# Layer 0's attention half a unit behind its maxima, in program order, with loads by need

## The chip, the cores and the metric

The kernel runs on one core of one Trainium2 chip. Times are device microseconds of one execution. A core has five engines with a queue each: TensorE (PE: matrix products, with its weight loads shown as PEld), VectorE (DVE), ScalarE (ACT), GpSimd (POOL) and SyncE (SP, which issues transfers). Products land in PSUM, a small memory of eight banks for each of 128 partitions; all other tiles lie in SBUF. An engine executes its own queue in order and waits for the others by semaphores.

## The reference

The program is a sequence of two transformer layers over x of 2 batches, 1024 tokens and 128 channels. Each part is added to x after a layernorm of x:

```
x = x + L0_attn(layernorm(x))   # 8 heads of 128, queries and keys through a latent of 32, rotary part of 32
x = x + L0_ffn(layernorm(x))    # a shared expert and the best 2 of 8 experts for each token
x = x + L1_attn(layernorm(x))   # 16 heads of 8, rotated, causal
x = x + L1_ffn(layernorm(x))    # 2 of 8 experts for each batch
```

The change lies in L0_attn. It is, with c_q and c_kv of 32 channels:

```
c_q, c_kv = h @ W_DQ + b_DQ, h @ W_DKV + b_DKV
q = [c_q @ W_UQ + b_UQ, c_q @ W_QR + b_QR];  k = [c_kv @ W_UK + b_UK, h @ W_KR + b_KR]
attn = softmax(q @ k.T / sqrt(160));  out = (attn @ v) @ W_O + b_O,  v = c_kv @ W_UV + b_UV
```

The kernel never builds the heads of 128 channels. It multiplies the weights with each other first: W_UQ with W_UK into `g`, a map from c_q to 64 channels per head, and W_UV with W_O into `w_vo`. Scores are then products over 64 channels, and values have 32.

## The kernel before

**Layer 0's attention** is cut into four units: 2 batches by 2 groups of 4 heads, `i = 0..3`. A unit has two passes over its 1024 by 1024 scores.

- `maxima0(i)` (L612) computes scores with queries on the partitions. A tile `sc` (L621) covers 128 queries, 512 keys and 2 heads: two matrix products on two halves of the rows of PE, then one `tensor_reduce` on DVE (L628). There are 32 tiles and 32 yields in a unit. After every 16 tiles the maxima are split into three bf16 parts on DVE (L640 to L653), and `rows` (L655) turns them into rows: 16 small products, and a copy to `mr` on ACT.
- `attend0(i)` (L670) computes the scores again, with keys on the partitions (L692), adds the negated maxima by a product with ones (L698), takes the exponential on ACT (L703), adds up the exponentials for the denominator (`sum`, L708 and L711: on POOL, for the last unit on DVE) and multiplies them with the values (`values`, L721) into `ud`. It also has 32 tiles and 32 yields, in two halves `c`. At the end of a half, `end` (L733) multiplies the sums with ones (`den`), copies `ud` and `den` on ACT, and puts six items into the list `late`: four divisions, a blank and `add`, the product with `w_vo` that goes into x. `run` (L677) takes one item before each yield.

In what follows a step is one yield of these generators.

Tiles `sc`, and all small products of this stage, share a PSUM pool `ps` of three buffers of two banks each (L466).

**Ahead of the units** stand `prepare(0)` (L545: layernorm, transposes, `cq`, `key2`, `val`, `cc`) and `queries(0)` (L594: two products of 33 rows, copied on ACT to `q2`). Before them in the program come the loads, the constants (masks, `tri`, `thr`, `ids` and others), and the products of weights: `gp` (L507), `vo` (L517) and `bo` (L527, with `bv` and `b_o` giving the output's bias `b_all`). x is loaded in four pieces by SP (L65), then the expert weights `wall` (L491 to L495); the other weights go through ACT's queue, the first five ahead of `w_up`, `w_o` and `g`.

**The order.** Five stages run (L779). Stage i takes a step of `maxima0(i)`, a step of `attend0(i - 1)` and a step of `more()` in turn, until all have ended; so stage 0 has maxima alone and stage 4 attention alone. `more()` prepares the second batch in stage 1, and makes the next queries, a piece every four steps. In stages 0 to 3 the order is fixed on PE alone; the order of the other engines, and everything ahead of stage 0, is up to a scheduler that plans with estimated times. In stage 4 PE, DVE, POOL and SP follow the program (`IN_ORDER`, L42), and `ahead` goes on by one step beside each: `route(0)` (L287), the choice of experts for the first batch, two of its yields at a time, then the gathers `get(0)` (L449) of the first rows for the experts. After that come the experts, layer 1's attention and its experts, which the change does not touch.

Of the kernel before, what the change touches and what calls it, by code (L numbers as in the profile page):

```python
# [13 lines left out]
F32 = mybir.dt.float32  # L14
# [7 lines left out]
P = 128  # L22
# [3 lines left out]
NE = 8  # L26
# [23 lines left out]
def two_layers(ctx: ExitStack, tc: tile.TileContext, a: dict, out: bass.AP):  # L50
# [13 lines left out]
    for i in range(4):  # L64
        nc.sync.dma_start(  # L65
            x[:, 4 * i : 4 * i + 4, :],
            a["h"][4 * i * P : 4 * (i + 1) * P, :].rearrange("(n p) d -> p n d", p=P),
        )

    ident = const.tile([P, P], F32, name="ident")  # L70
# [3 lines left out]

    mask_st = const.tile([P, P], BF16, name="mask_st")
    nc.gpsimd.memset(mask_st, 0.0)
    nc.gpsimd.affine_select(
        out=mask_st, in_=mask_st, compare_op=ALU.is_ge, fill=MASKED,
        base=0, pattern=[[-1, P]], channel_multiplier=1,
    )  # L80
    mask_ts = const.tile([P, P], BF16, name="mask_ts")
    nc.gpsimd.memset(mask_ts, 0.0)
    nc.gpsimd.affine_select(
        out=mask_ts, in_=mask_ts, compare_op=ALU.is_ge, fill=MASKED,
        base=0, pattern=[[1, P]], channel_multiplier=-1,
    )
    mhalf = const.tile([P, NT], F32, name="mhalf")
    nc.gpsimd.memset(mhalf, -0.5)

    rev_i = const.tile([P, NE], I32, name="rev_i")  # L90
    nc.gpsimd.iota(rev_i, pattern=[[-1, NE]], base=NE, channel_multiplier=0)
    rev = const.tile([P, NE], F32, name="rev")
    nc.vector.tensor_copy(rev, rev_i)

    end_i = const.tile([P, 1], I32, name="end_i")
    nc.gpsimd.iota(end_i, pattern=[[0, 1]], base=NE * P, channel_multiplier=1)
    row_end = const.tile([P, 1], F32, name="row_end")
    nc.vector.tensor_copy(row_end, end_i)

    def load(name, shape, src):  # L100
        t = const.tile(shape, F32, name=name)
        nc.scalar.dma_start(t, src)
        return t

    w_lat = load("w_lat", [P, 160], a["w_lat"])
    b_q = load("b_q", [DC, 1], a["b_q"])
    b_kr = load("b_kr", [P, 1], a["b_kr"])
    b_v = load("b_v", [P, DC], a["b_v"].partition_broadcast(P))
    b_o = load("b_o", [P, D], a["b_o"].partition_broadcast(P))

# [118 lines left out]
    def beside(main, extras, ends=False):  # L229
# [20 lines left out]

    tri = rt.tile([P, P], BF16, name="tri")
    nc.gpsimd.memset(tri, 1.0)
    nc.gpsimd.affine_select(
        out=tri, in_=tri, compare_op=ALU.is_gt, fill=0.0,
        base=0, pattern=[[1, P]], channel_multiplier=-1,
    )
    onesq = rt.tile([P, P], BF16, name="onesq")
    nc.vector.memset(onesq, 1.0)

    before = rt.tile([P, NE, NE], F32, name="before")  # L260
    nc.gpsimd.memset(before, 1.0)
    nc.gpsimd.affine_select(
        out=before, in_=before, compare_op=ALU.is_gt, fill=0.0,
        base=0, pattern=[[1, NE], [-1, NE]], channel_multiplier=0,
    )
    def counted(name, shape, pattern, by_partition=0):
        t = rt.tile(shape, F32, name=name)
        i = rt.tile([P, P], I32, name="counted")
        n = 1
        for k in shape[1:]:  # L270
            n *= k
        nc.gpsimd.iota(i[:, 0:n], pattern=pattern, base=0, channel_multiplier=by_partition)
        nc.vector.tensor_copy(t if len(shape) == 2 else t.rearrange("p a b -> p (a b)"), i[:, 0:n])
        return t

    thr = counted("thr", [P, NE, NT], [[0, NE], [P, NT]])
    nth = counted("nth", [P, NBLK], [[1, NBLK]])
    col = counted("col", [P, P], [[1, P]])
    ids = counted("ids", [P, 2, NT], [[0, 2], [P, NT]], 1)

    PAD = 4
    cums = [rt.tile([P, PAD + NT, NE], BF16, name=f"cum{i}") for i in range(4)]
    for t in cums:
        nc.vector.memset(t[:, 0:PAD], 0.0)
# [179 lines left out]
    with ExitStack() as att:  # L464
# [21 lines left out]
        w_o = q_pool.tile([P, H0, D], F32, tag="q2", name="w_o")  # L486
        nc.scalar.dma_start(w_o, a["w_o"].rearrange("(h d) e -> d h e", d=P))

        g = wa.tile([DA, H0, DC + DR], F32, name="g")
        nc.scalar.dma_start(g[:, :, DC : DC + DR], a["w_qr"])  # L490
        nc.sync.dma_start(wall[:, :, 0:FF], a["ffn_gate"])  # L491
# [4 lines left out]
        gate_w = load("gate_w", [P, NE], a["gate_w"])  # L496
        w_qkv = load("w_qkv", [P, 3 * D], a["w_qkv"])
        w_out1 = load("w_out1", [P, D], a["w_out"])
        w_rot = load("w_rot", [P, 2 * D], a["w_rot"])
        w_r = load("w_r", [P, NE], a["w_r"])  # L500
        b_r = load("b_r", [P, NE], a["b_r"].partition_broadcast(P))
# [3 lines left out]
        gp = ps.tile([P, H0, DA], F32, tag="ps", name="gp")  # L505
        for h in range(H0):
            nc.tensor.matmul(  # L507
                gp[:DA, h, :], w_up[:, 0, h, :], w_up[:, 1, h, :], start=True, stop=True
            )
        nc.vector.tensor_copy(g[:, :, 0:DC], gp[:DA, :, 0:DC])  # L510
        nc.vector.tensor_scalar(gc, gp[:DA, :, DC], QSCALE, None, ALU.mult)

        vo = ps.tile([P, 2, D], F32, tag="ps", name="vo")
        for hg in range(2):
            for j in range(4):
                h = 4 * hg + j
                nc.tensor.matmul(  # L517
                    vo[DC * j : DC * (j + 1), hg, :], w_up[:, 2, h, 0:DC], w_o[:, h, :],
                    start=True, stop=True,
                )  # L520
        nc.vector.tensor_copy(w_vo, vo)

        bv = q_pool.tile([P, H0, P], F32, tag="q2", name="bv")
        nc.vector.tensor_copy(bv, w_up[:, 2, :, DC : DC + 1].to_broadcast([P, H0, P]))
        bo = ps.tile([P, D], F32, tag="ps", name="bo")
        for h in range(H0):
            nc.tensor.matmul(  # L527
                bo, bv[:, h, :], w_o[:, h, :], start=(h == 0), stop=(h == H0 - 1)
            )
        b_all = wa.tile([P, D], F32, name="b_all")  # L530
        nc.vector.tensor_tensor(b_all, bo, b_o, ALU.add)


        onesb = wa.tile([P, P], BF16, name="onesb")
        nc.vector.memset(onesb, 1.0)
        ones32 = wa.tile([P, DC], F32, name="ones32")
        nc.vector.memset(ones32, 1.0)

        mps = [wa.tile([P, 4, 4, 64], BF16, name=f"mp{i}") for i in range(2)]
        for t in mps:  # L540
            nc.gpsimd.memset(t, 0.0)
        mrs = [wa.tile([P, 2, S], BF16, name=f"mr{i}") for i in range(2)]
        ctx_b, qs, last_rows = {}, {}, {}

        def prepare(b):  # L545
# [3 lines left out]
            yield from layernorm_steps(b, bank0, xt, xn)  # L549
# [17 lines left out]
            nc.vector.tensor_scalar(key2, pk, b_kr, None, ALU.add)  # L567
            yield
            val = lat.tile([P, NT, DC], F32, name="val")
# [9 lines left out]

            cc = lat.tile([P, H0, NT], F32, name="cc")  # L580
# [5 lines left out]
            nc.vector.tensor_copy(cc.rearrange("p h n -> p n h"), pc)  # L586
            nc.gpsimd.tensor_tensor(
# [3 lines left out]
            ctx_b[b] = (cq, key2, val, cc)  # L591
# [78 lines left out]
        def attend0(i):  # L670
# [11 lines left out]
            for c in range(2):  # L682
                cols = slice(512 * c, 512 * (c + 1))
                ud = None
                sums = []
                for k in range(NT):
                    es = []
                    for pr in range(2):
# [16 lines left out]

                        if k == 1:
                            t = s_pool.tile([P, 2, 512], F32, name="sum")
                            adder.tensor_tensor(t, before[pr], ex, ALU.add)  # L708
                            sums.append(t)
                        elif 1 < k < NT - 1:  # L710
                            adder.tensor_tensor(sums[pr], sums[pr], ex, ALU.add)  # L711
# [16 lines left out]
                    if c == 0 and k == 1:  # L728
                        last_rows.pop(i)()
# [3 lines left out]
                def end(c=c, ud=ud, sums=sums, es=es, values=values):  # L733
# [30 lines left out]

                    for n in range(4):
                        late.append(lambda n=n: divide(n))
# [7 lines left out]
        for _ in prepare(0):  # L774
            pass
        for _ in queries(0):
            pass
        n = 2 * B
        for i in range(n + 1):  # L779
            passes = []  # L780
            if i < n:
                passes.append(maxima0(i))
            if i:
                passes.append(attend0(i - 1))
            if i == n:

                ahead = chain(hurry(route(0, bank0, spare0), 2), get(0))

            def more():
                if i == 1:  # L790
                    yield from prepare(1)
                if i + 1 < n:
                    yield from queries(i + 1)

            passes.append(spread(more(), 4))
            if i < n:
                with tc.manual_schedule(engines={mybir.EngineType.PE}):
                    for _ in zip_longest(*passes):
                        pass
# [694 lines left out]
```

## Time and profile before

| | us |
|---|---|
| median of the 3 runs | 1014.03 (1010.83 to 1015.8) |
| the profiled execution | 1025.0 |
| its span, first to last instruction | 1023.2 |
| PE busy | 909.4 (89%) |
| DVE busy | 587.9 (57%) |
| ACT busy | 424.2 (41%) |
| POOL busy | 414.9 (41%) |

The profile is one execution, and it took 1% longer than the median. Its page lists, among others, the chain of work that ended last (PE has 66% of it, DVE 17%) and the costliest groups of instructions. For layer 0's attention these are:

| line | engine, what | instructions | busy us | mean ns |
|---|---|---|---|---|
| L624 | PE, scores for the maxima | 512 | 149.4 | 637 |
| L628 | DVE, maxima of a tile | 128 | 153.8 | 1219 |
| L692 | PE, scores again | 512 | 141.3 | 616 |
| L698 | PE, maxima added | 256 | 51.6 | 382 |
| L703 | ACT, exponentials | 128 | 131.0 | 1023 |
| L711 | POOL, sums | 60 | 140.1 | 2349 |
| L723 | PE, values | 512 | 69.5 | 615 |

A product of 32-bit numbers counts as two instructions on PE. Products overlap each other, so a group's busy time is less than its count by its mean. Lines of the order in time give start, length, engine, source line, operation, output and input with their shapes, the count, and in brackets how long the engine stood idle before and what ended that. The granted clock is PE's: 1.00 is full speed, 0.50 half.

### The profile page before, as it was taken

How to read it: one execution, taken by the hardware profiler on the slowest of the kernel's cores; microseconds unless marked ns; L12 is line 12 of the kernel's file. 1: busy time of each engine (PE TensorE's matmuls, PEld its weight loads, DVE VectorE, ACT ScalarE, POOL GpSimd, SP SyncE). 2: the span in 40 equal slices, each digit the busy share in tenths (PEclk: the TensorE clock that was granted, in tenths of full speed). 3: DMA queues.
4: the chain of work that ended last, by engine and by line, in shares of the span. 5: the costliest groups of instructions: out<-in, count | busy, mean ns of one | idle time of the engine just before them, and what ended most of it. 6: DMA issues, size and time to landing. Idle time of an engine off the chain costs nothing.

```text
span 1023.2 us, 14408 instructions
## 1 busy us (share of the span) xinstructions
PE 909.4 (89%) x5308; PEld 438.3 (43%) x5308; DVE 587.9 (57%) x1085; ACT 424.2 (41%) x694; POOL 414.9 (41%) x532
## 2 busy tenths in 40 slices
PE   3998999999999998999798996779889999899974
PEld 2533433333333333336675575433344445444333
DVE  4496454546564657746633573746755777467322
ACT  0102334444334344454231352224646765576741
POOL 2003727373846550265047510156672234144320
PEclk9799999999999999999899997859897998789987
DMA  9000000000000000014122233332312222120000
GB/s 277 15 1 1 1 2 1 1 1 1 1 2 1 1 1 21 6 34 92 26 60 29 39 69 84 70 49 35 83 36 59 33 36 32 35 40 13 3 0 21
DMA packets 34874, 33.49 MB, mean 33 GB/s; under 512 B 5804, under 2 KB 32332, under 8 KB 33644
## 3 DMA queue, kind: packets, MB, share of 16 engines
q1 hardware_dynamic: 24978, 24.09, 10.4%
q0 software_dynamic: 6592, 5.91, 4.1%
q10 hardware_dynamic: 3235, 2.58, 1.0%
q8 instruction: 43, 0.70, 0.3%
q14 instruction: 26, 0.21, 0.1%
HBM read 24.10 MB, written 8.45 MB: 32 GB/s over the span
## 4 chain that ended last, share of the span: by engine, by line
PE 66%; DVE 17%; issue 4%; DMA 4%; POOL 4%; ACT 4%; SPq 0%; POOLq 0%; ACTq 0%; DVEq 0%
PE sc L692 10%; PE sc L624 8%; PE up L1252 7%; PE ud L723 6%; PE banks L1112 5%; PE bank L1227 4%; DVE mx2a L628 4%; PE gub L880 4%; DVE rden L750 3%; DVE mx L1122 2%; PE sc L698 2%; PE gu L834 2%; PE yblk L908 2%; ACT ex L1232 1%; PE banks L1029 1%
## 5 line engine op out<-in xcount | busy, mean ns | idle before, releaser
L1122 DVE TENSOR_REDUCE mx<-banks 128x2 f32<-128x1024 f32 (+3 forms) x160 | 174.0, 1113 | 92.0 <-PE banks L1117 72.0
L628 DVE TENSOR_REDUCE mx2a<-sc 128x2 f32<-128x1024 f32 x128 | 153.8, 1219 | 113.3 <-PE sc L624 100.7
L703 ACT ACTIVATE ex<-sc 128x1024 f32<-128x1024 f32 x128 | 131.0, 1023 | 211.9 <-PE sc L698 208.8
L1232 ACT ACTIVATE ex<-bank 128x512 f32<-128x512 f32 (+2 forms) x320 | 155.9, 559 | 125.3 <-PE bank L1227 121.8
L711 POOL TENSOR_TENSOR sum<-sum,ex 128x1024 f32<-128x1024 f32 x60 | 140.1, 2349 | 38.0 <-ACT ex L703 38.0
L624 PE MATMUL sc<-key,q 64*128 64x512 f32 x512 | 149.4, 637 | 1.2 <-DVE mx2a L628 1.1
L692 PE MATMUL sc<-q,key 64*128 64x512 f32 x512 | 141.3, 616 | 8.6 <-DVE mx2a L628 8.4
L1112 PE MATMUL banks<-kp,qp 72*128 72x512 bf16 (+3 forms) x384 | 111.4, 362 | 18.3 <-DVE mx L1122 9.9
L1227 PE MATMUL bank<-qp,kp 75*128 75x512 bf16 (+3 forms) x384 | 100.5, 347 | 4.5 <-ACT ex L1232 2.8
L1236 POOL TENSOR_SCALAR_AFFINE_SELECT ex<-ex 128x128 f32<-128x128 f32 (+1 forms) x192 | 63.9, 368 | 89.3 <-ACT ex L1232 85.0
L456 POOL DMA_INDIRECT xb<-xn,row x46 | 53.0, 1152 | 103.0 <-DVE fblk L432 42.5
L1252 PE MATMUL up<-ex,vp 128*32 128x512 f32 (+3 forms) x768 | 85.6, 540 | 3.9 <-POOL ex L1236 3.9
L938 POOL DMA_INDIRECT x<-ys,pos x32 | 49.9, 1559 | 82.7 <-DMA kp<-parts 65.8
L692 PEld LDWEIGHTS sc<-q,key 64*128 64x128 f32 x512 | 49.6, 191 | 74.7 <-issue 43.1
L624 PEld LDWEIGHTS sc<-key,q 64*128 64x128 f32 x512 | 48.1, 190 | 73.5 <-issue 49.8
L723 PE MATMUL ud<-ex,val 128*32 128x512 f32 x512 | 69.5, 615 | 0.0
L1112 PEld LDWEIGHTS <-qp 72*128 72x128 bf16 x384 | 40.1, 107 | 66.2 <-issue 51.8
L880 PE MATMUL gub<-wall,xbt 128*128 x184 | 66.2, 486 | 1.8 <-ACT xbt L867 1.3
L708 POOL TENSOR_TENSOR sum<-ex,ex 128x1024 f32<-128x1024 f32 x12 | 28.2, 2347 | 74.2 <-ACT ex L703 74.2
L886 DVE TENSOR_TENSOR hds<-slb,gub 128x352 f32<-128x352 f32 x46 | 23.8, 517 | 57.0 <-ACT slb L885 56.8
L1117 PE MATMUL banks<-mask_st,identb 128*128 128x128 bf16 x256 | 53.5, 237 | 0.0
L698 PE MATMUL sc<-mr,onesb 64*128 64x512 bf16 x256 | 51.6, 382 | 0.0
(264 smaller groups left out, 1105.4 us busy)
## 6 DMA issues: line engine op xcount, KB each, us to landing
qp<-parts SPq DMA_DIRECT2D x72, 64.0 KB
kp<-parts SPq DMA_DIRECT2D x72, 64.0 KB
parts<-qk SPq DMA_DIRECT2D x24, 128.0 KB
ys<-yb SPq DMA_DIRECT2D x10, 256.0 KB
wall<-in_ffn_gate_dram SPq DMA_DIRECT2D x1, 1584.0 KB
wall<-in_ffn_up_dram SPq DMA_DIRECT2D x1, 1584.0 KB
wall<-in_ffn_down_dram SPq DMA_DIRECT2D x2, 576.0 KB
x<-in_h_dram SPq DMA_DIRECT2D x4, 256.0 KB
```

The costliest lines, as they stand in the source:

```text
L624: nc.tensor.matmul(sc[:, j, :], qs[i][pr][r, st * P : (st + 1) * P], key2[r, 512 * c : 512 * (c + 1)], start=True, stop=True,)
L628: nc.vector.tensor_reduce(mx2[:, 2 * pr : 2 * pr + 2, st, c], sc, AX.X, ALU.max, negate=True,)
L692: nc.tensor.matmul(sc[:, j, :], key2[r, k * P : (k + 1) * P], qs[i][pr][r, cols], start=True, stop=False,)
L703: nc.scalar.activation(ex, sc, AF.Exp)
L711: adder.tensor_tensor(sums[pr], sums[pr], ex, ALU.add)
L723: nc.tensor.matmul(ud[DC * j : DC * (j + 1), :], val[:, k, :], es[j // 2][:, j % 2, :], start=(k == 0), stop=(k == NT - 1),)
L880: nc.tensor.matmul(gu[:, s, 0:FF], xbts[j // 4][:, (j % 4) * P : (j % 4 + 1) * P], flat[:, bass.ds(e0 + FF * s, FF)], start=True, stop=True,)
L1112: nc.tensor.matmul(sc[:, n, 0:w], qp[0:KP, j, s0 : s0 + P], kp[0:KP, j, c0:c1], start=True, stop=not diag,)
L1122: nc.vector.tensor_reduce(to, sc[:, :, 0:w], AX.X, ALU.max, negate=True)
L1227: nc.tensor.matmul(sc[:, j, 0:w], kp[0 : KP + 3, j0 + j, t0 : t0 + P], qp[0 : KP + 3, j0 + j, lo:hi], start=True, stop=True,)
L1232: nc.scalar.activation(ex[:, :, 0:w], sc[:, :, 0:w], AF.Exp, scale=SCALE1)
L1252: nc.tensor.matmul(up[WH * j : WH * (j + 1), lo - c0 :], vps[b][:, k, h : h + WH], es[j], start=(k == 0), stop=end,)
```

## The change

Nothing of the computation changes but the order, the queues and the engine of some small copies.

- **Loads.** Only the first two pieces of x (the first batch) are loaded at the start. ACT's queue gets `w_up` first, then `w_lat`, `b_q`, `b_kr`, an exponential of one column (`warm`), `g`, `b_v`, `b_o`. SP gets `w_o`, the second batch's x, `wall`, and then the weights of later stages, which ACT had.
- **The start.** Layernorm of the first batch; then `products()`, the eight products of `gp` and their copies to `g` and `gc`; then transposes, `cq`, `key2`; then `queries(0)`; then the constants. Conversions of constants from integers go from DVE to POOL. An unused mask is gone. All this is in program order on PE, DVE, POOL and SP.
- **Small products among the first maxima.** `val`, `cc`, `vo` and `bo` become four pieces of `prepare(0)`, at steps 0, 4, 8 and 12 of the first unit, the bias of x at 16, queries(1) at 20 and 24.
- **Half a unit behind.** The four maxima passes follow each other without a break, as one generator of 128 steps. Attention, one generator too, begins 23 steps after them (`LAG`), so both run together for 105 steps, and attention is alone for 23, where before it was 96 and 32. The second batch is prepared in fine pieces from step 32 on.
- **Program order** holds on PE, DVE, POOL and SP for all of it. `ahead` begins at step 117, two steps before the last attention unit.
- **In `attend0`** the adding of a tile is issued after the exponential of the next one (`due`), the last rows are made at k = 6 of the first half and not at k = 1, and a blank stands ahead of the divisions.

```diff
@@ loads @@
-    for i in range(4):
+    def load_x(i):
         nc.sync.dma_start(
...
+    for i in range(2):
+        load_x(i)
...
         nc.scalar.dma_start(w_up, a["w_up"])
-        w_o = q_pool.tile([P, H0, D], F32, tag="q2", name="w_o")
-        nc.scalar.dma_start(w_o, a["w_o"].rearrange("(h d) e -> d h e", d=P))
+        w_lat = load("w_lat", [P, 160], a["w_lat"])
+        b_q = load("b_q", [DC, 1], a["b_q"])
+        b_kr = load("b_kr", [P, 1], a["b_kr"])
+
+        warm = small.tile([P, 1], F32, name="warm")
+        nc.vector.memset(warm, 0.0)
+        nc.scalar.activation(warm, warm, AF.Exp)
...
+        b_v = load("b_v", [P, DC], a["b_v"].partition_broadcast(P))
+        b_o = load("b_o", [P, D], a["b_o"].partition_broadcast(P))
+        w_o = q_pool.tile([P, H0, D], F32, tag="q2", name="w_o")
+        nc.sync.dma_start(w_o, a["w_o"].rearrange("(h d) e -> d h e", d=P))
+        for i in range(2, 4):
+            load_x(i)
...
-        gate_w = load("gate_w", [P, NE], a["gate_w"])
+        gate_w = load("gate_w", [P, NE], a["gate_w"], nc.sync)
...
@@ prepare @@
-            yield from layernorm_steps(b, bank0, xt, xn)
+            yield from layernorm_steps(b, bank0, xt, xn, fine=b > 0)
...
+            yield
+            if b == 0:
+                yield from output()
             nc.gpsimd.tensor_tensor(
...
@@ attend0 @@
+                        if due:
+                            due.pop()()
                         if k == 1:
-                            t = s_pool.tile([P, 2, 512], F32, name="sum")
-                            adder.tensor_tensor(t, before[pr], ex, ALU.add)
-                            sums.append(t)
-                        elif 1 < k < NT - 1:
-                            adder.tensor_tensor(sums[pr], sums[pr], ex, ALU.add)
+                            sums.append(s_pool.tile([P, 2, 512], F32, name="sum"))
+                        if 0 < k < NT - 1:
+                            a1 = before[pr] if k == 1 else sums[pr]
+
+                            def add_up(t=sums[pr], a1=a1, ex=ex):
+                                adder.tensor_tensor(t, a1, ex, ALU.add)
+
+                            due.append(add_up)
...
-                    if c == 0 and k == 1:
+                    if c == 0 and k == 6:
                         last_rows.pop(i)()
...
+                    late.append(lambda: None)
                     for n in range(4):
                         late.append(lambda n=n: divide(n))
@@ the order @@
+        UNIT, LAG = 4 * NT, 2 * NT + 7
+        start = prepare(0)
...
+        def more():
+            ahead = prepare(1)
+            for i in range(n):
+                now = chain(
+                    start if i == 0 else ahead if i == 1 else (),
+                    queries(i + 1) if i + 1 < n else (),
+                )
+
+                first = 16 if i == 1 else 0
+                yield from padded(chain(islice(now, first), spread(now, 2 if first else 4)), UNIT)
+
+        with tc.manual_schedule(engines=IN_ORDER):
+            next(start)
+            products()
+            for _ in islice(start, 2):
+                pass
+            for _ in queries(0):
+                pass
...
+        passes = zip_longest(
+            chain(*map(maxima0, range(n))), after(LAG, chain(*map(attend0, range(n)))), more()
+        )
+        with tc.manual_schedule(engines=IN_ORDER):
+            for _ in islice(passes, (n - 1) * UNIT + LAG - 2):
+                pass
+
+            ahead = chain(hurry(route(0, bank0, spare0), 2), get(0))
+            for _ in passes:
+                next(ahead, None)
```

`padded(steps, n)` fills a generator up to n yields with blanks. `products()` holds the lines of `gp`, `g` and `gc` as they were, and `output()` those of `vo`, `bv`, `bo` and `b_all`, each with a yield behind it.

## The prediction

> **What bounds the kernel now.** I read the page's slices first, then busy time by stretches cut at layer 0's stages, then the order of instructions in time, then the waits.
>
> ```profile
> PE   3998999999999998999798996779889999899974
> ...
> PEclk9799999999999999999899997859897998789987
> ```
>
> Layer 0 ends near 456 us, so it fills the first 18 digits. TensorE stands at 9 except at the start. The stretches are the start, a slow-clock piece, the first maxima alone, maxima beside attention, and the last attention alone (columns: length, then PE, PEld, DVE, ACT and POOL busy, clock, DMA share, GB/s):
>
> ```profile
> 0.00:34.00 34.00, 16.15 (x98) 11.53 (x99) 19.13 (x92) 2.46 (x3) 9.60 (x28) 1.00 0.80 219
> 34.00:47.00 13.00, 13.00 (x23) 5.68 (x23) 1.53 (x2) 3.07 (x3) 0.00 (x0) 0.50 0.00 1
> 47.00:84.00 37.00, 35.00 (x144) 11.92 (x142) 35.84 (x39) 2.04 (x2) 0.00 (x0) 1.00 0.00 0
> 84.00:374.00 290.00, 281.32 (x1612) 106.42 (x1608) 161.37 (x212) 114.34 (x118) 170.66 (x73) 0.99 0.00 1
> 374.00:456.00 82.00, 75.51 (x479) 29.54 (x471) 56.53 (x119) 38.88 (x43) 22.53 (x21) 0.96 0.06 17
> ```
>
> The start is half idle on PE. In 34 to 47 PE is full, but at half clock. In 47 to 84 DVE is full. From 84 on it is PE. The instructions in order of time say why the start is slow (start, length, engine):
>
> ```profile
> 11.09 0.69 DVE L524 COPY bv<-w_up 128x1024 f32<-128x1024 f32 x1 [2.82 <-DMA w_up<-in_w_up_dram]
> ...
> 18.09 1.08 PE L517 MATMUL vo<-w_o,w_up 128*32 128x128 f32 x16 [5.87 <-DMA w_o<-in_w_o_dram]
> ...
> 19.24 0.42 DVE L521 COPY w_vo<-vo 128x256 f32<-128x256 f32 x1 [5.45 <-PE vo L517]
> ...
> 68.47 16.11 DVE L628 TENSOR_REDUCE mx2a<-sc 128x2 f32<-128x1024 f32 x14
> ```
>
> DVE stands 2.82 us for `w_up`, then 5.45 us for a product that waits for `w_o`; behind it stands the layernorm that feeds all else. The reductions alone come every 16.11/14 = 1.15 us. Beside attention, PE sets the step:
>
> ```profile
> 207.62 1.06 PE L723 MATMUL ud<-ex,val 128*32 128x512 f32 x8
> 208.62 1.13 PE L624 MATMUL sc<-key,q 64*128 64x512 f32 x4
> ...
> 209.58 1.02 PE L692 MATMUL sc<-q,key 64*128 64x512 f32 x4
> ...
> 210.44 0.38 PE L698 MATMUL sc<-mr,onesb 64*128 64x512 bf16 x2
> 210.75 1.16 PE L756 MATMUL y<-w_vo,ot 128*128 128x128 f32 x8
> ...
> 211.84 1.13 PE L624 MATMUL sc<-key,q 64*128 64x512 f32 x4
> ```
>
> From start to start: a maxima tile 0.96, an attention tile 0.86 + 0.31, values 1.00 every second step, an output product 1.09. So a step of both costs 0.96 + 1.17 + 0.50 = **2.63 us**, attention alone 1.67, maxima alone 1.15 (DVE).
>
> **The sum of before**, by the profiled execution (1025.0 us, span 1023.2; the median of the runs shown is 1014.03, 1.1% less, so I carry a difference over as it is). Maxima begin at 38.9 us and run alone to 83.5 (44.6 us); both run to 374.4 (290.9); attention alone to 455.6 (81.2); the rest is 567.6. A test of the step prices on the middle: 96 x 2.63 = 252.5, and on PE beside them second-batch preparation 8.6 (transposes 1.2, 1.83, 1.91, 1.90, 1.77), four query products of 1.71 = 6.8, five denominators of 1.8 = 9.0, five outputs 5.5, six row products of 0.62 = 3.7: 286.1 against 290.9, so 4.8 are stalls. The last stage: 32 x 1.67 = 53.4, denominators 5.4, outputs 2.2, route(0) 8.2, rows 0.6: 69.8 against 81.2. 11.4 are lost there: two dips to half clock of 3.4 us each cost 3.4, PE's waits for route's DVE chain 3.3 and for `ot` 2.5.
>
> **Part 1, the start.** The first two `x` loads (512 KB), `w_up` (396) and `w_lat` (80) now go first: 0.99 MB, where before it was the four `x` loads, whose last rows reached DVE at about 8 us; so stats end at 8.0 (estimate). The DVE order is now by hand: 15 dependent small operations at 0.20 each (as at 28 to 29 us) give 11.0, eight `xn` at 0.24 give 12.9. From the copy of the first `xt` half, 12.3 by then, to the end of `pk` took 25.01 to 29.72 = 4.7, giving 17.0. `gp` (1.1 on PE), `g` and `gc` (0.55 on DVE) lie before that in PE's and DVE's idle time, for which `w_up` need only land by 11. Then queries(0): eight records.
>
> Here the trace and a rule differ. The eight records took 0.85 each, because the clock was 0.50 while PE was 13.00 of 13.00 us busy. The Trainium skill (TensorE: Matmul & The Clock Gate, Part 1) says that the array starts at half rate, goes to full after about 3.4 us of sustained work, and falls back after an idle window of that length. By the rule the queries, following `pcq` and `pk` without a gap, run at full rate: 8 x 0.43 = 3.5. By the row they stay slow (their operands have 33 rows of 128): 6.8. The same rule speaks against the change: `vo` and `bo` kept PE at work from 18.1 to 22.9 ahead of `pcq`; now nothing does, and `pcq` + `pk` (3.8 at full clock) may take up to 7.5. So maxima begin between 17.0 + 3.5 = 20.6 and 17.0 + 3.7 + 6.8 = 27.6. I take **24.5**, as if one of the two pieces were slow: 14.4 earlier than before.
>
> The constants that move to Pool (some 6 us) and the six small memsets on DVE fall in waits for PE; without that cover DVE would pay about 0.8. SP and ACT only issue the moved loads, 0.3 to 0.5 each: `x` of the second batch and `wall` start later by one issue, and wanted are they from step 32 and after layer 0. `w_o` reached PE at 18.1; it is now wanted at step 8, near 35, and the small weights behind `wall` only from route on. The early exponential hides its 1.28 us table load before 12 us.
>
> **Part 2, maxima alone, now 23 steps** with `pv`, `pc`, `vo`, `bo` among them: 23 x 1.15 = 26.5. The small products were on PE before, so this is work moved, not removed. From below: PE has 23 x (1.15 - 0.96) = 4.4 us to spare against about 7.3 of products, so 2.9. From above, nothing hidden: 1.9 + 1.9 + 1.1 + 3.8, `bv` 0.7, evacuations 1.4 = 10.8. I take 7.3: `pv` at step 0 has no backlog to cover it (1.9), `pc` and `vo` are half covered (1.4), and `bo` waits for `bv` behind a reduction while the next reduction waits for `bo` (4.0). Row splitting 1.3, rows and the first query of unit 1 1.2, first tiles at half clock 2: **38** in all.
>
> **Part 3, both, 105 steps instead of 96.** 105 x 2.63 = 276.2, beside it the 33.6 of before plus a query 1.7, a denominator 1.8, an output 1.1, rows 0.6 and route's transposes and logits 3.9: 318.9. Stalls: the pairs of divisions at once (two reciprocals 1.76 ahead of a reduction, five times) go, as each step now holds one division (0.95 + 0.28), and half a unit of lag puts them 7 steps away from the row splitting. What is late next: steps 117 to 127, where maxima(3), attention's sums on DVE (1.2 each), four divisions and route's first DVE work meet. DVE 12.7 + 8.4 + 4.9 + 0.7 + 11 + 2 = 40 against PE's 36 (28.9 and 1.8 + 1.1 + 3.9 of the extras). I put these 4 as all that is lost: **323**. Queries(2) at steps 56 and 58 take query buffers free since 54; the last rows, now at k = 6, are wanted four steps on. Both cost nothing. `pcq` and `pk` of the second batch put 2.5 us of DVE ahead of one reduction; at once.
>
> **Part 4, attention alone, 23 steps.** 38.4, two denominators 3.6, an output 1.1, rows 0.6, route's rest 4.3 = 48.0. Of the 11.4 lost I keep 8.4; adding a tile one step late spares DVE waits for ACT (10.4 + 3.9 us before), though DVE is not the bound there: **56.4**. Route leads the end by 34 steps instead of 32, so the first gathers keep their 27 us before the experts.
>
> **Sum:** 24.5 + 38 + 323 + 56.4 = 441.9 against 455.6: 13.7 less. The rest stays at 567.6. The median follows: 1014.0 - 13.7 = **1000**.
>
> **Where it could go otherwise.** About 0.5% (5 us) is what can be told from no change.
>
> *Half of it* (1007): the clock stays slow until after the first tiles (27.6), and the products cost 10.8: 3.1 + 3.5 given up. For it: the row of 0.50. Against: queries(1) now come at step 20 and not among the first tiles, where they held the clock down.
>
> *More* (990): warm at 20.6 (3.9), products at 2.9 (4.4), no stalls in part 3 (2): 10 more. Against it: `bo`'s serial wait.
>
> *Slower* (1020): DVE in program order becomes the bound where units meet.
>
> ```profile
> DVE mx2a L628 <- PE sc L624: 99.9, 71, 3.3
> ...
> PE sc L692 <- DVE mx2a L628: 8.4, 10, 2.0
> ```
>
> In 84 to 374 (us in total, times, longest) reductions wait long for PE and PE little for them: the reduction of 209.79 ended at 211.02, and its buffer was wanted at 212.80, so a margin of 1.8 us. In steps 117 to 127 a step has reduction 1.15, sum 1.2, division 1.2, route 1.0 = 4.6, and in order behind them waits for Pool's inverse root (382.09 to 386.40, 4.3) and PE (3.3): 11 x 4.6 + 7.6 = 58, and a PE left waiting so drops to half clock once more (1.7, as at 405): 60 against the 40 in my sum. 20 lost outweigh 13.7. It decides from 59 us on in those steps; against it, not every step has all four, and their true sum is 40.
>
> **Chances.** The forecast 0.54, half 0.20, more 0.09, slower 0.17. Faster: 0.52 + 0.12 + 0.09 = 0.73; within 0.5%: 0.12 (half's tail 0.08, edges 0.04); slower 0.15. The range reaches from 990 (more) to 1012 (half, with 5 us of stalls in part 3); the slower rival lies outside.
>
> **What would show it.** First maxima matmul between 20.6 and 27.6; first L692-kind tile 36 to 41 us later; layer 0's last denominator near 442; reductions' idle time still ended by PE; from there on 568 us. It is wrong if PE waits for reductions by more than 20 us in all, if steps 117 to 127 take over 50 us, or if the rest of the kernel changes by over 5 us.

## The result and the profile after

The changed kernel is **0.55% slower**: 1020.84 us (median of 13 runs) against 1014.97 (13 runs), ratio 1.0055 with a 95% interval of 1.0033 to 1.0077. The forecast was 1.4% faster, and the range (990 to 1012) does not hold the time.

The spans of the two profiled executions say the opposite, 1015.1 after against 1023.2 before. That must not be read as a gain. Behind layer 0 the code is the same, and there the profile of before took 567.6 us; the profiles of the changed kernel and of ten variants took 551.9 to 565.8. Before and after differ there by 14.9 us, and the granted clock fits that: 0.89 on average in the one and 0.92 in the other, some 61 and 46 us lost. So the stretch to compare is layer 0, from the start to its last denominator: 455.6 us before, **462.4** after, 6.8 later, which fits the medians' 5.9.

These are the stretches of the changed kernel's layer 0 by busy time (columns: start and end, length, PE, PEld, DVE, ACT, POOL, clock, DMA share, GB/s): the start, maxima alone, both, attention alone.

```profile
0.00:23.00 23.00, 11.90 (x39) 5.25 (x40) 11.06 (x51) 3.67 (x5) 7.35 (x30) 1.00 0.98 289
23.00:60.30 37.30, 31.84 (x182) 16.60 (x180) 28.78 (x36) 3.07 (x4) 2.35 (x1) 1.00 0.13 23
60.30:403.50 343.20, 318.79 (x1792) 124.77 (x1792) 223.97 (x290) 126.91 (x133) 174.76 (x80) 0.97 0.01 2
403.50:461.00 57.50, 53.40 (x323) 21.36 (x323) 40.88 (x81) 26.46 (x28) 16.77 (x15) 0.88 0.06 15
```

The start and maxima alone came out as forecast: 60.3 us against 62.5. Both passes together took 343.2 where the forecast had 323, and the clock there is 0.97. (The 1.00 of the start covers only its end: the trace's first clock record is of 18.3 us.) The waits of the stretch 60 to 404 (us in total, times, longest) name who is late:

```profile
PE sc L641 <- DVE mx2a L577: 18.5, 6, 3.8
...
PE sc L573 <- DVE mx2a L577: 5.0, 5, 2.5
```

PE stands 23.5 us for reductions, in 11 places, where before it was 8.4 in 10 (the prediction's line for 84 to 374). One such place, DVE alone, in order of time: the last reduction of 16, the splitting of the maxima into rows, the next reduction.

```profile
197.26 1.23 DVE L577 TENSOR_REDUCE mx2a<-sc 128x2 f32<-128x1024 f32 x1 [0.38 <-PE sc L573]
198.53 0.18 DVE L589 TENSOR_TENSOR m<-mx2a 128x16 f32<-128x16 f32 x1
198.74 0.17 DVE L594 TENSOR_TENSOR m<-m,cc 128x16 f32<-128x16 f32 x1
198.94 0.17 DVE L595 TENSOR_TENSOR m<-m,cc 128x16 f32<-128x16 f32 x1
199.15 0.20 DVE L598 CAST mp<-m 128x16 bf16<-128x16 f32 x1
199.39 0.18 DVE L601 TENSOR_TENSOR mq<-m,mp 128x16 f32<-128x16 f32 x1
199.61 2.37 DVE L598 CAST mp<-mq 128x16 bf16<-128x16 f32 x1
202.02 2.24 DVE L601 TENSOR_TENSOR mq<-mq,mp 128x16 f32<-128x16 f32 x1
204.29 0.20 DVE L598 CAST mp<-mq 128x16 bf16<-128x16 f32 x1
204.38 1.22 DVE L577 TENSOR_REDUCE mx2a<-sc 128x2 f32<-128x1024 f32 x1
```

The cast of 16 elements takes 0.20 at 199.15 and 2.37 at 199.61. POOL, in the same microseconds:

```profile
193.41 4.67 POOL L663 TENSOR_TENSOR sum<-sum,ex 128x1024 f32<-128x1024 f32 x2 [0.34 <-ACT ex L652]
199.56 4.66 POOL L663 TENSOR_TENSOR sum<-sum,ex 128x1024 f32<-128x1024 f32 x2 [1.49 <-ACT ex L652]
```

POOL is idle from 198.08 to 199.56, and all operations of DVE in that gap are short. Its next sum runs from 199.56 to 201.9: the cast issued just behind it ends at 201.98. The second sum runs to 204.22: the subtraction issued in it ends at 204.26. So the slow operations seem not to work for 2.3 us: each waits for one sum of POOL and shows the wait as its duration. The experiments test this reading. PE pays twice, as its rows show:

```profile
205.65 1.76 PE L573 MATMUL sc<-key,q 64*128 64x512 f32 x4 [2.52 <-DVE mx2a L577]
207.19 1.92 PE L641 MATMUL sc<-q,key 64*128 64x512 f32 x4
```

It stands 2.52 us, and the tile of 207.19 then takes 1.92 instead of 1.02, because the granted clock fell to half at 206.0 for 3.4 us.

Before the change the same splitting stood here:

```profile
186.70 0.21 DVE L649 CAST mp<-m 128x16 bf16<-128x16 f32 x1
...
187.40 0.18 DVE L652 TENSOR_TENSOR mq<-mq,mp 128x16 f32<-128x16 f32 x1
187.62 0.20 DVE L649 CAST mp<-mq 128x16 bf16<-128x16 f32 x1
...
199.01 2.36 POOL L708 TENSOR_TENSOR sum<-ex,ex 128x1024 f32<-128x1024 f32 x1 [14.25 <-ACT ex L703]
```

Nothing is slow, for POOL stood idle for 14.25 us until 199.01. Sums exist for k = 1 to 6 of each attention half only, so POOL is free around the change of halves. Before, a splitting fell exactly there. Half a unit behind, it falls on k = 4 of a half, in the middle of the sums.

### The profile page after: what moved, and what is told of

Read it like the earlier page. It is cut to its first block, busy times and chain, and to the rows that moved or that the text cites. A ratio compares the mean times of both kernels' runs of the same rounds, so it can differ in the third digit from the quotient of the medians.

```text
span 1015.1 us, 14402 instructions
## 1 busy us (share of the span) xinstructions
PE 893.1 (88%) x5308; PEld 434.7 (43%) x5308; DVE 617.5 (61%) x1080; ACT 423.8 (42%) x695; POOL 413.1 (41%) x536
## 4 chain that ended last, share of the span: by engine, by line
PE 64%; DVE 21%; issue 5%; POOL 4%; ACT 3%; DMA 3%; SPq 0%; POOLq 0%; ACTq 0%; DVEq 0%
PE sc L573 9%; PE sc L641 9%; PE up L1284 7%; PE ud L677 5%; PE banks L1144 4%; DVE mx2a L577 4%; PE bank L1259 4%; PE gub L912 4%; DVE mx L1154 2%; PE sc L647 2%; PE gu L866 2%; DVE mp L598 2%; PE yblk L940 2%; DMA kp<-parts 2%; PE banks L1061 1%
## 5 line engine op out<-in xcount | busy, mean ns | idle before, releaser
L641 PE MATMUL sc<-q,key 64*128 64x512 f32 x512 | 147.5, 635 | 18.9 <-DVE mx2a L577 18.5
L573 PE MATMUL sc<-key,q 64*128 64x512 f32 x512 | 146.7, 631 | 7.7 <-DVE mx2a L577 7.7
L1144 PE MATMUL banks<-kp,qp 72*128 72x512 bf16 (+3 forms) x384 | 107.6, 352 | 17.8 <-DVE mx L1154 10.9
L1259 PE MATMUL bank<-qp,kp 75*128 75x512 bf16 (+3 forms) x384 | 97.9, 339 | 4.8 <-ACT ex L1264 2.5
L641 PEld LDWEIGHTS sc<-q,key 64*128 64x128 f32 x512 | 52.4, 197 | 83.3 <-issue 41.0
L1144 PEld LDWEIGHTS <-qp 72*128 72x128 bf16 x384 | 38.9, 104 | 63.3 <-issue 48.0
L647 PE MATMUL sc<-mr,onesb 64*128 64x512 bf16 x256 | 54.5, 394 | 0.0
```

The lines of the kernel that those rows point to most:

```text
L573: nc.tensor.matmul(sc[:, j, :], qs[i][pr][r, st * P : (st + 1) * P], key2[r, 512 * c : 512 * (c + 1)], start=True, stop=True,)
L641: nc.tensor.matmul(sc[:, j, :], key2[r, k * P : (k + 1) * P], qs[i][pr][r, cols], start=True, stop=False,)
L1144: nc.tensor.matmul(sc[:, n, 0:w], qp[0:KP, j, s0 : s0 + P], kp[0:KP, j, c0:c1], start=True, stop=not diag,)
L1259: nc.tensor.matmul(sc[:, j, 0:w], kp[0 : KP + 3, j0 + j, t0 : t0 + P], qp[0 : KP + 3, j0 + j, lo:hi], start=True, stop=True,)
```

## The experiments

Three theories were set against each other. **P**: DVE's small operations wait for POOL's sums. **O**: program order on DVE makes the reductions late, with or without POOL. **J**: the loss is in steps 117 to 127, where the slower rival of the prediction had it. A fourth, **C**, is about PE's clock in the start.

The table gives each run's ratio to the kernel before on its own chip (the chips' medians of before went from 1015 to 1028, so only ratios compare), and from its profile the first maxima tile, the first attention tile and the end of layer 0 in us.

| run | ratio (95%) | maxima | attention | layer 0 ends |
|---|---|---|---|---|
| before | 1 | 37.9 | 83.5 | 455.6 |
| the change | 1.0055 (1.0033 to 1.0077) | 23.1 | 60.3 | 462.4 |
| no_sums | 0.9678 (0.9643 to 0.9713) | 22.0 | 61.5 | 424.1 |
| split_pool | 0.9802 (0.9751 to 0.9854) | 22.5 | 58.2 | 432.5 |
| lag32 | 0.9809 (0.9759 to 0.9859) | 22.7 | 70.9 | 433.9 |
| order_pe | 0.9979 (0.9954 to 1.0004) | 22.9 | 57.1 | 453.9 |
| small_first | 1.0102 (1.0036 to 1.0167) | 27.2 | 67.1 | 471.1 |
| before_split | 0.9970 (0.9936 to 1.0004) | 39.2 | 83.9 | 454.1 |
| split_norm_pool | 0.9660 (0.9619 to 0.9701) | 23.0 | 58.6 | 424.5 |
| route_early | 0.9647 (0.9595 to 0.9698) | 23.2 | 58.8 | 422.2 |
| lag32_norm | 0.9691 (0.9659 to 0.9723) | 23.2 | 69.8 | 431.0 |
| bias_early | 0.9606 (0.9584 to 0.9628) | 22.4 | 60.1 | 423.4 |

**no_sums: take POOL's work away.** The sums take in 8 of 512 columns; the rest of the denominators is left out.

```diff
-                            def add_up(t=sums[pr], a1=a1, ex=ex):
-                                adder.tensor_tensor(t, a1, ex, ALU.add)
+                            def add_up(t=sums[pr], a1=a1, ex=ex, k=k):
+                                if k == 1:
+                                    adder.memset(t, 1.0)
+                                w = slice(0, 8)
+                                adder.tensor_tensor(t[:, :, w], a1[:, :, w], ex[:, :, w], ALU.add)
```

> The changed kernel with POOL's sums (and the last unit's on DVE) cut to 8 of 512 columns; the rest of the denominators is left out and stands at 1. Theory P (DVE's row splitting and second-batch layernorm wait while POOL adds, because both read SBUF through something they share): the cast and subtract of the splitting, 1.1 and 1.56 us on average in the changed kernel, fall to 0.2; the step after each splitting falls from 6.7-8.2 us to about 3.1; both passes together fall from 343 us to 318 or less and layer 0 ends near 435 instead of 462. Theory O (program order on DVE makes the reductions late, whatever POOL does): the slow steps stay over 6 us, layer 0 ends within 5 us of 462, less the DVE time saved in the last unit. Theory J (the loss is in steps 117 to 127, where the last unit's sums on DVE, route and maxima meet): only those steps get shorter, by some 10 us.

Layer 0 ended at 424.1, 11 us better than P's number. DVE kept its order and its splittings, and their casts came down from 969 ns (shown under lag32) to 210:

```profile
L598 DVE CAST mp<-mq 128x16 bf16<-128x16 f32 x14 | 2.9, 210 | 0.5
```

The step behind a splitting, from one attention tile to the next, took 3.13 us (four of seven; the second, 6.7, and the third, 4.1, hold products of the second batch, the last, 4.4, route). That is P, and against O and J. Part of the gain is not P's: the last unit's sums were cut on DVE as well.

**split_pool: move the splitting to POOL, behind its sums.** Seven operations of a splitting move; the eighth, the minimum, stays on DVE and becomes a `tensor_reduce`.

```diff
-                    nc.vector.tensor_tensor(
-                        m4, mx2[:, :, sts, 0], mx2[:, :, sts, 1], ALU.min
-                    )
+                    nc.vector.tensor_reduce(m4, mx2[:, :, sts, :], AX.X, ALU.min)
...
-                    nc.vector.tensor_tensor(m4, m4, ch, ALU.subtract)
-                    nc.vector.tensor_tensor(m4, m4, ch, ALU.add)
+                    nc.gpsimd.tensor_tensor(m4, m4, ch, ALU.subtract)
+                    nc.gpsimd.tensor_tensor(m4, m4, ch, ALU.add)
...
-                        nc.vector.tensor_copy(mp[:, :, :, k], m4)
+                        nc.gpsimd.tensor_copy(mp[:, :, :, k], m4)
...
-                            nc.vector.tensor_tensor(r, m4, mp[:, :, :, k], ALU.subtract)
+                            nc.gpsimd.tensor_tensor(r, m4, mp[:, :, :, k], ALU.subtract)
```

> The changed kernel with the row splitting (subtract, add, casts, subtracts) on POOL behind its sums, and its minimum as a reduction on DVE. Theory P: DVE's slow casts and subtracts are gone, the steps after the splittings fall to about 3.1-4 us, seven times 3.5 us and the half clock behind them come back: layer 0 ends near 437, the whole some 25 us below the changed kernel, so near 995; what is left is the second batch's layernorm. Theory O: no change, as DVE is still in order; within 5 us of the changed kernel. Theory J: no change.

432.5, some 5 us better than P's number. Nothing but the place of seven small operations and the form of the minimum differs, and all their results have 16 elements a partition. The stretch of both passes, by busy time:

```profile
58.20:373.80 315.60, 307.12 (x1792) 121.85 (x1792) 191.76 (x247) 126.56 (x133) 183.61 (x122) 1.00 0.01 3
```

315.6 us against 343.2, at full clock throughout. The steps behind the first six splittings were 7.1, 7.4, 8.2, 6.7, 6.7, 6.7 us in the changed kernel and are 3.1, 6.7, 4.1, 3.1, 3.1, 3.1 here. By the rows, the 27.6 us have two parts. PE's idle time fell from 24.4 us to 8.5, which is 15.9. Its busy time for the same 1792 records fell from 318.8 to 307.1, which is 11.7: the changed kernel ran 23.9 us of this stretch at half clock, split_pool none, and half of 23.9 is 12.

**lag32: put the splittings back where POOL is idle, with all else of the change kept.**

```diff
-        UNIT, LAG = 4 * NT, 2 * NT + 7
+        UNIT, LAG = 4 * NT, 4 * NT
```

(The buffer `bv` is taken ahead of the queries, so that buffers come free in time.)

> The changed kernel with attention a whole unit (32 steps) behind the maxima, as before the change; start, program order and small products stay. The splittings then fall on the first steps of an attention half, when POOL has no sums. Theory P: casts and subtracts at 0.2 us, as before the change; layer 0 ends 14 us before 455.6 less what the small products cost in the start, so near 443, and the whole near 1003. Theory O: the steps stay slow, layer 0 ends at 460 or later. Theory J: route again begins when maxima are over, some 10 us better than 462.

The splitting by groups over all of layer 0's attention, first in the changed kernel, then here (count, busy us, mean ns):

```profile
L598 DVE CAST mp<-mq 128x16 bf16<-128x16 f32 x14 | 13.6, 969 | 0.5
L601 DVE TENSOR_TENSOR mq<-mq,mp 128x16 f32<-128x16 f32 x7 | 9.5, 1360 | 0.2
```

```profile
L598 DVE CAST mp<-mq 128x16 bf16<-128x16 f32 x14 | 2.9, 205 | 0.5
...
L601 DVE TENSOR_TENSOR mq<-mq,mp 128x16 f32<-128x16 f32 x7 | 1.3, 185 | 0.2
```

The same operations, still in program order on the same engine, take a fifth and a seventh of the time where they stand beside an idle POOL. Layer 0 ends at 433.9, 9 us better than expected. The later adding (`due`) and the last rows at k = 6 are kept in this run, so the loss is not theirs.

**order_pe: undo program order on DVE, POOL and SP** for steps 0 to 116.

```diff
-        with tc.manual_schedule(engines=IN_ORDER):
+        with tc.manual_schedule(engines={mybir.EngineType.PE}):
             for _ in islice(passes, (n - 1) * UNIT + LAG - 2):
```

> The changed kernel with program order on PE alone for steps 0 to 116; from 117 on as it was. Theory P: the splittings still fall beside POOL's sums, the casts stay slow, layer 0 ends within 6 us of 462. Theory O: layer 0 ends 15 to 20 us earlier. Theory J: no change.

453.9: 8.5 us earlier, between what P and O expected. Casts were still slow (736 to 898 ns on average), and PE still stood 21.6 us for reductions ahead of L641. And the 8.5 us do not lie where O had them. From the first attention tile to the end of the last maxima tile, the changed kernel first, then order_pe:

```profile
60.33:401.76 341.43, 317.02 (x1784) 124.14 (x1784) 222.41 (x283) 126.34 (x132) 174.76 (x80) 0.97 0.01 2
57.11:398.65 341.54, 315.49 (x1784) 121.31 (x1784) 205.84 (x262) 126.34 (x132) 173.07 (x79) 0.98 0.01 2
```

Both take the same time. 3.2 us were won ahead of this stretch, most of it between maxima tiles 12 and 13 (2.9 us for 5.7), where the scheduler makes `bv` earlier. The other 5.4 were won behind it, with 10.2 us less of half clock, worth up to 5.1. The `xn` of the second batch were faster too (335 ns on average over both batches, for 722), but that did not shorten the stretch. So program order has a cost in the maxima alone; in the stretch that failed no cost of it can be seen.

**before_split: the control.** The edit of split_pool in the kernel before.

> The kernel before with the row splitting on POOL and its minimum as a reduction, nothing else. Theory P: before the change the splittings stand where POOL has no sums, so the casts were at 0.2 us; moving them wins at most the 0.5 us of DVE time that PE sees at a half's end: ratio to before 0.995 to 1.003. If the splitting on DVE were costly in itself, the gain would be that of the changed kernel, 0.975 or better.

0.9970, with 1 inside the interval. Where the splitting met no sums, moving it is worth nothing that can be told.

**small_first: narrow products back ahead of the queries.**

```diff
-            for _ in islice(start, 2):
+            for _ in islice(start, 4):
                 pass
```

> The changed kernel with the products of val and cc back ahead of the queries, as before the change; the rest stays. They are 32 and 8 columns wide. Theory C (a stretch of such narrow products takes PE's clock to half, and the queries of 33 rows keep it there): a piece of half clock of 7 to 14 us appears within 10 us of the queries, the queries take 0.85 us a record again and not 0.43-0.47, and the first maxima tile moves from 23.1 to 30 us or later, that is by the 3.7 us of the two products and over 3 us of clock. If the half clock of the kernel before came from something else, only the 3.7 us: about 26.8. In both cases the first attention tile moves less than that, as two pieces are gone from among the maxima.

First small_first, then the changed kernel, from 20 us on (the clock is the third column from the end):

```profile
20.00:24.00 4.00, 4.00 (x34) 3.82 (x33) 1.95 (x4) 0.00 (x0) 0.00 (x0) 1.00 1.21 275
24.00:28.00 4.00, 4.00 (x8) 1.72 (x8) 0.43 (x8) 1.02 (x1) 0.00 (x0) 0.65 0.83 151
28.00:32.00 4.00, 4.00 (x24) 1.46 (x22) 1.09 (x1) 1.02 (x1) 0.00 (x0) 0.50 0.01 4
```

```profile
20.00:24.00 4.00, 4.00 (x13) 1.87 (x12) 1.70 (x8) 1.32 (x2) 0.00 (x0) 1.00 1.22 269
24.00:28.00 4.00, 4.00 (x27) 2.75 (x26) 2.11 (x3) 0.73 (x1) 0.00 (x0) 1.00 0.85 152
28.00:32.00 4.00, 4.00 (x28) 2.63 (x26) 4.00 (x4) 0.00 (x0) 0.00 (x0) 1.00 0.02 4
```

PE is full in all six rows, yet in small_first the clock fell to half at 25.2 for 10.2 us, right behind the narrow products. The first maxima tile came at 27.2, where C had expected 30 or later and its rival 26.8: the queries suffered only in their second half, and by this number alone C would have lost. Half clock of 10 us or more ahead of 60 us was seen in all three profiles with the narrow products first (before 13.7, before_split 13.7, small_first 10.2), and in one of nine with them behind (bias_early, 10.2, from 23.0 on, ahead of its first narrow product at 24.5). So the association is strong, but C is not settled: the drop does not need them. Nor does it need queries(1) among the first tiles, which the prediction held to be what kept the clock down: small_first has none there.

**split_norm_pool: take the other clash away too.** split_pool, with the inverse root (`pool=`) and the `tensor_scalar` for `xn` (`by=`) of the second batch on POOL.

```diff
-            yield from layernorm_steps(b, bank0, xt, xn, fine=b > 0)
+            yield from layernorm_steps(
+                b, bank0, xt, xn, fine=b > 0, pool=b > 0, by=nc.gpsimd if b else None
+            )
```

> The changed kernel with the row splitting on POOL and the second batch's inverse root and normalising on POOL too, so that no small DVE operation stands against POOL's sums but the divisions. Theory P: the stalls left in the second unit (steps of 6.5, 4.0 and 3.3 us where PE's work gives 3.1 and 2.3) fall by 4 us together; layer 0 ends near 428.5 against 432.5 with the splitting alone. If POOL becomes late with its sums, the denominators wait and layer 0 ends later than 432.5.

424.5: 8 us for the expected 4. The step of 6.5 us is 3.1. In the stretch of order_pe's rows, no_sums first, then this run:

```profile
61.48:368.31 306.83, 304.68 (x1784) 121.57 (x1784) 185.69 (x285) 126.32 (x132) 31.95 (x91) 1.00 0.01 3
58.63:365.36 306.73, 305.11 (x1784) 121.46 (x1784) 177.50 (x218) 126.30 (x132) 192.45 (x136) 1.00 0.01 3
```

PE is idle for 1.6 us of it, and the stretch is as short with all of POOL's sums (this run) as without them (no_sums). So it was the meeting that cost, not the sums, and what no_sums had saved on DVE in the last unit does not show here.

**route_early: theory J at last.** split_norm_pool, with route from step 100 on, one piece a step.

```diff
-            for _ in islice(passes, (n - 1) * UNIT + LAG - 2):
+            for _ in islice(passes, 100):
                 pass
 
-            ahead = chain(hurry(route(0, bank0, spare0), 2), get(0))
+            ahead = chain(route(0, bank0, spare0), get(0))
```

> As the run with splitting and normalising on POOL, and route begins at step 100, one of its pieces a step, where it began at 117 with two. Theory J (the meeting of maxima, route and the sums on DVE costs 8 to 10 us at the end): the slow steps between attention tiles 97 and 115 (5.0, 4.3, 5.5, 8.8, 6.3 us) shrink, layer 0 ends 5 to 8 us earlier. If they come from route's own chain of answers between engines, they only move, within 2 us.

422.2: 2.4 us, just over the 2 of a mere move and short of J's 5 to 8, and the ratio does not tell it from split_norm_pool. Layer 0 also had 6.8 us less of half clock, worth up to 3.4, so the clock may be all of it. The stretch of both grew from 306.7 to 313.3 us while attention alone shrank: the work moved forward and stayed. J is out, as a loss of its own.

**lag32_norm: what half a unit is worth by itself.** split_norm_pool with the edit of lag32.

> The run with splitting and normalising on POOL, with attention a whole unit behind (32 steps) and not 23: what half a unit is worth when nothing of the splitting meets POOL's sums on DVE. By the sum of the prediction nine tiles of maxima leave the stretch where they cost 1.15 us and go where they cost 0.96, which is 1.7 us, and two route steps more lead the end: layer 0 ends 0 to 4 us later than 424.5. If lagging by half a unit were the larger part of the gain, it ends over 8 us later.

431.0 against 424.5, between the two expectations; the intervals of the ratios overlap. It had 3.4 us more of half clock, worth up to 1.7, so half a unit is worth some 5 us in the profile.

**bias_early: the lowest ratio.** route_early with the copy `bv` made by POOL in the start.

> The fastest run so far (route at step 100) with the broadcast copy for the output bias made by POOL at the start and not by DVE among the first maxima. The 5.7 us between maxima tiles 12 and 13 fall to about 3.0, as the product no longer waits for the copy behind a reduction; the first attention tile 2 to 2.7 us earlier, and the end of layer 0 the same. If DVE had a backlog to catch up with anyway, under 1 us.

Between maxima tiles 12 and 13 it was 2.9 us and no longer 5.7, as expected. The first attention tile came 1.2 us later, though, and not 2 to 2.7 earlier: the profile has 10.2 us of half clock from 23.0 on. Over five runs it stands at 986.99 us against 1027.87 before on its chip, 3.9% faster than before; its interval overlaps that of route_early.

## Why the prediction was wrong

**The start was right.** Forecast 24.5, measured 23.1. (Before, the first maxima matmul stands at 37.9 and not at the 38.9 of the prediction, so the gain is 14.8 us against a forecast of 14.4.) One of `pcq` + `pk` and the queries was taken as slow, and one was, but the other way round than the row of half clock suggested: `pcq` took 3.62 us behind an idle PE (1.90 before), and the eight queries came 0.44 us apart (0.80 before). So the rule of the clock told the order rightly, slow first and then full; but full clock was granted at 18.3, 6.1 us after PE had resumed at 12.2, where the rule as the prediction gives it has about 3.4. The row's half clock did not come with the queries; small_first got part of it back with the narrow products, as said above.

**Maxima alone were right**: 38 against 37.2 (23.1 to 60.3), with `bo` at 5.7 us between two tiles as the largest piece.

**Both passes hold the error**: 20.2 of the 20.5 us by which layer 0 ended later than forecast. The step that failed is the stalls: "I put these 4 as all that is lost", all of it in steps 117 to 127. PE's idle time was 343.2 - 318.8 = 24.4 us, 23.5 of it waits for reductions, which is over the 20 that the prediction itself named as a sign of being wrong. Behind it stands "half a unit of lag puts them 7 steps away from the row splitting". That looked at one neighbour, the divisions on the same engine, and not at the other, POOL's sums on the next engine. The row splitting has a price in maxima alone (1.3 us) and none beside attention. In the rows of before it takes 1.75 us (186.07 to 187.82), just inside the margin of 1.8 that the prediction had read itself; two waits of some 2.1 us take it far outside. The forecast put a stall-free place where the change had in fact moved the splitting out of the quiet time.

A second term was put at nothing, and luck hid it. The sum for PE's work, 318.9, looks exact beside the measured 318.8, but the measured time contains the half clock. At full clock the same 1792 records took 307.1 us (split_pool). So the work was priced some 12 us too high, and half clock, 11.7 by this comparison, was put at nothing in this part. The test of the step prices on before had the same flaw: it gave 286.1 of work and 4.8 of stalls for 290.9, while the prediction's own row for 84 to 374 has PE busy for 281.3 of 290 us, with two pieces of half clock, of 3.4 us each, among them.

The trace of before had the evidence, in two rows of the start that the prediction does not use:

```profile
25.73 2.35 POOL L587 TENSOR_TENSOR x<-x,b_all 128x1024 f32<-128x1024 f32 x1 [1.33 <-DVE rstd L163]
25.90 2.21 DVE L162 SCALAR_TENSOR_TENSOR fix<-fix,var 128x8 f32<-128x8 f32 x1
```

An operation on 8 elements that takes 0.17 at 28.54 takes 2.21 here and ends, at 28.1, with POOL's. The Trainium skill states the rule (SBUF — State Buffer, Who interferes with whom): VectorE and GpSimd share a pair of SBUF ports, held by one of them for a whole instruction, and on VectorE it is casts, copies and `tensor_scalar` that can ask for it, and operations with two SBUF inputs beside a GpSimd operation that reads SBUF. The runs agree with who waits: casts, subtractions and `xn` do, while the changed kernel's 128 reductions from PSUM stay between 1193 and 1228 ns whatever POOL does. That the ports are what they wait for is the page's word; the runs show only that the wait ends with POOL's operation.

**Attention alone** took 58.9 us (403.5 to 462.4) against 56.4: two pieces of half clock of 6.8 us each in place of 3.4, so 3.4 us more.

**The rivals.** The slower one had the right mechanism in part, a DVE in order that is late, and the right sign, but the wrong place and cause: steps 117 to 127 took 35.7 us against PE's 36 in the sum. That its 1020 is the measured time is luck. The loss was spread over the splittings and the second batch's layernorm. The rest of the kernel changed by more than the 5 us that were named as a sign, but not with the change: before_split, whose code there is that of before, took 553.9.

## What to carry to other kernels

When a change moves work in time, ask what runs beside it in the new place on the engine that shares its memory path, not only what stands in the same queue. A tiny operation that takes ten times its usual time and ends together with a large one on the neighbour is likely a wait; look for such rows before taking a duration as a price. And an operation that was cheap only because its neighbour paused must keep its place, or go to that neighbour's queue: seven small operations moved to POOL turned a loss of 0.55% into a gain of 2.0%.

## What the runs showed of the hardware

Stalls often cost PE twice. Beside attention the changed kernel has six waits of PE of 2.5 us or more (2.5 to 3.8). Around the end of five of them the clock fell to half, for 3.4 or 6.8 us, as at 206.0 with the wait of 2.52; with the sixth (3.37 us, ending at 306.7) it did not, nor with one of 3.19 us in split_pool (ending at 117.7). So these runs give no length of a wait that is safe, and none that is sure to cost.

The clock also fell while PE showed no idle time, 1.5 us behind products of 32 and 8 columns (small_first, 25.2), and in the three profiles with these products first it stayed at half for 10.2 to 13.7 us; in one of the nine starts without them ahead it did so too.

A small operation of DVE that stands beside POOL's sums can take ten times as long (a cast of 16 elements 2.37 us for 0.20), and in the profile the wait looks like work.
